# Layer 0 of a graph network: relations of three slots in four by matmul, a multiplied chunk last in each tile, and the tile's end ahead of the counts

## The chip, the cores and the metric

The kernel runs on one core of a Trainium2 chip. The metric is the device time of one launch in microseconds (us), as the median of several runs. Beside these runs there is one profiled execution, from which the trace and the profile page come. A measurement of the kernel before varies by about 0.3%.

## The reference, cut to what matters

Four graph layers follow one another on 3125 nodes of 128 features, with the same 100000 edges (src to dst), each layer added to its input and normalised. The change is in the first layer (L0), an attention over incoming edges whose logits and messages also depend on the type of the edge, one of 500 relations:

```python
z_bar = segment_sum(z[edge_type], dst) / max(deg, 1)
pre_edge = hP1[dst] + hP2[src] + zP3[edge_type]          # 128 wide
logit_edge = leaky(pre_edge) @ y_w                       # 8 heads
pre_self = hP1 + hP2 + z_bar @ P3;  logit_self = leaky(pre_self) @ y_w
alpha = softmax over self and incoming edges, per dst and head
t_edge = hWh[src] + zWz[edge_type];  t_self = hWh + z_bar @ Wz
out = leaky(segment_sum(alpha * t, dst) + residual_weight * h)   # h where deg == 0
```

Layer 1 is a mean over neighbours followed by two dense layers. Layers 2 and 3 are further attentions over the same edges.

## The kernel before, in words

**Tiles and slots.** Nodes are sorted by in-degree and cut into 25 tiles of 128 nodes, one node to a partition. Tile t has CAP[t] slots (57 in the first tile, 21 in the last, 821 in all); slot s of a tile holds the s-th incoming edge of each of its nodes. A chunk is W = 8 slots; the last chunk of a tile is shorter where CAP is not a multiple of 8.

**Gathers.** For each slot one indirect DMA on POOL (helper line L90) fetches 128 rows of `h_tab`, one per node: the row of the source node with its part of the pre-activation (128 columns), its message (128) and 8 logit columns, 264 f32 in all. They land in `hs`, a buffer of one chunk, of which there are eight. So a tile of four chunks has two generations of buffers.

**Two ways to the relation's part.** `gathered` (L820 to 835) fetches for each slot also 128 rows of `z_tab` by an indirect DMA into `zs` (328 columns, two buffers), adds `zs` to `hs` on DVE (L826), and sums the 64 raw relation columns by halving (L814, L817) into the tile's sum `za` (L828). `multiplied` (L837 to 875) fetches no relation rows. It loads the relation numbers of the chunk broadcast over the partitions (`rb`, 256 KB, a DMA on the SP queue, L843), compares them on DVE with the four blocks of relation ids (L852, `oh`, one-hot), multiplies the one-hots with the table of relations `zq` on PE (L854, `zps`), copies the product to `zT` on ACT (L856), and adds the relation's part by further matmuls: into `pre` (L858) and, by `t_ps` (L866), on DVE into `hs` (L867). The sum over the chunk's slots goes to `zbT` (L870 and the halving helper, L874). In both ways `pre` is completed by the node's own part (L799) and by transposes of the gathered rows (L833, L860), passed through a Relu on ACT (`low`, L806), and turned into logits by a small matmul for each slot (L808).

**Which chunks are multiplied.** `by_matmul(t)` takes about 45% of a tile's slots, in full chunks spread over the tile from slot 0 on; the tile's last chunk is a gathered one in most tiles. Over all tiles 47 chunks (376 slots) are multiplied and 445 slots have a `zs` gather.

**The end of a tile.** When all chunks have logits, `masked` adds the parts of the logits into `lgs` (L881, L882), `softmax` takes maximum, exponentials and sums (L680 to 692), `faded` (L697) rescales, and `spread` (L886 to 891) weighs each chunk's messages in its `hs` buffer, sums them by halving and adds them into `az`. Only then is an `hs` buffer free. After that come the node's own term, layer normalisation (L724 to 735) and the stores of `x1_tab` (POOL, L93) and `u_tab` (SP, L1008).

**The counts.** Between the chunks, a generator `counts` (L563 to 645) is advanced step by step. It builds, for layer 1, the matrix of edge counts of a tile: compares on DVE (L559 through the helper `one_hots`, L608), scalings on ACT (L612, L613), matmuls on PE (L616, L634), copies on ACT (L636) and a store on SP (L643). The main loop does not need its results.

**The order.** The Python loop issues the tiles one after another and, ahead of a tile's last chunk, the `prologue` of the next one (its `x` was fetched by `own` a tile earlier). A scheduler then lays out the instructions for each engine by priority, which follows the order of issue; each engine runs its own list in order. SP's list holds the loads of `rb`, of the tile's sums (L771) and the stores; POOL's list holds all gathers.

Of the kernel before, what the change touches and what calls it, by code (L numbers as in the profile page):

```python
# [18 lines left out]
P = 128  # L19
N = 3125  # L20
NT = 25
# [6 lines left out]
W = 8  # L28
# [5 lines left out]
H = 8  # L34
R = 64
HC = 2 * D + H
NK = (PADREL + 1) // P
# [3 lines left out]
CAP = [57, 42, 40, 39, 38, 37, 36, 35, 35, 34, 33, 33, 32, 31, 31, 30, 30, 29, 28, 28, 27, 26, 25, 24, 21]  # L41
assert len(CAP) == NT
OFF = [sum(CAP[:t]) for t in range(NT + 1)]
# [7 lines left out]
NB = [3] * 3 + [2] * (NT - 4) + [1]  # L51
CW = 512
NCW = -(-NP // CW)


def chunks(t):
    return [(s, min(W, CAP[t] - s)) for s in range(0, CAP[t], W)]
# [7 lines left out]
    return [(run[0][0], sum(run[-1]), run) for run in runs]  # L65


def by_matmul(t):

    full = CAP[t] // W  # L70
    n = (9 * CAP[t] + 10 * W) // (20 * W)
    return {i * full // n * W for i in range(n)}


@with_exitstack
def tile_gnn(ctx, tc, a, out):
# [409 lines left out]
    with tc.tile_pool(name="srcp", bufs=1) as sp, tc.tile_pool(name="srcq", bufs=2, space=PSUM) as ps:  # L486
# [28 lines left out]
        for o in range(0, NS, P):  # L515
            n = min(P, NS - o)
# [15 lines left out]
        blk0[nb] = late.tile([P, NT], F32, name=f"blk0_{nb}")  # L532
        G.iota(blk0[nb], pattern=[[nb * P, NT]], base=0, channel_multiplier=0, allow_small_or_imprecise_dtypes=True)
    SG = 8
    SE = max(NB) * CW // P
    each_j = slots.tile([P, NT, max(CAP)], BF16, name="each_j")
    V.tensor_copy(each_j, digits[:, :NT].unsqueeze(2).to_broadcast([P, NT, max(CAP)]))
    NAX = NT * max(NB)
# [16 lines left out]
    def one_hots(to, nums, n, up):  # L555

        for i, k, w in ((0, n // 2, 2), (n - n % 2, n % 2, 1)):
            if k:
                V.tensor_tensor(to[:, i // 2:i // 2 + k, :, :w], nums[:, i:i + k * w]  # L559
                                .rearrange("p (b w) -> p b w", w=w).unsqueeze(2).to_broadcast([P, k, P, w]),  # L560
                                up[:, :, :w].unsqueeze(1).to_broadcast([P, k, P, w]), op=OP.is_equal)

    def counts(t, cp, ps, up):  # L563
# [57 lines left out]
        cs = cp.tile([P, NP], BF16, name="c_sb")  # L621
        for c in range(NCW):
            w = min(CW, NP - c * CW)
            n2, e0 = nb * w // P, nb * CW // P * c
            yield
            ohs = cp.tile([P, SE // 2, P, 2], BF16, name="c_ohs", bufs=2)
            ohd = cp.tile([P, SE // 2, P, 2], BF16, name="c_ohd", bufs=2)
            for to, end in ((ohs, 0), (ohd, 1)):
                one_hots(to, ends[:, end, e0:e0 + n2], n2, up)
            cps = ps.tile([P, CW], F32, name="c_ps")  # L630
            for j in range(w // P):
                for i in range(nb):
                    b = nb * j + i
                    T.matmul(cps[:, j * P:(j + 1) * P], ohd[:, b // 2, :, b % 2], ohs[:, b // 2, :, b % 2],  # L634
                             start=(i == 0), stop=(i == nb - 1))
            A.activation(cs[:, c * CW:c * CW + w], cps[:, :w], AF.Copy)  # L636
        yield
        od_ps = ps.tile([P, NT], F32, name="c_od", tag="c_ps")
# [36 lines left out]
    def softmax(pool, lg, n, heads, m, l, ex=None):  # L675


        ex = lg if ex is None else ex
        mx = pool.tile([P, heads], F32, name="mx")
        V.tensor_reduce(mx, lg.rearrange("p s h -> p h s"), AX.X, OP.max)  # L680
        mn = pool.tile([P, heads], F32, name="mn")
        V.tensor_max(mn, m, mx)
        corr = pool.tile([P, heads], F32, name="corr")
        V.tensor_sub(corr, m, mn)
        A.activation(corr, corr, AF.Exp)
        V.tensor_copy(m, mn)
        V.tensor_sub(lg, lg, mn.unsqueeze(1).to_broadcast([P, n, heads]))
        A.activation(ex, lg, AF.Exp)
        sm = pool.tile([P, heads], F32, name="sm")
        V.tensor_reduce(sm, ex.rearrange("p s h -> p h s"), AX.X, OP.add)  # L690
        V.tensor_mul(l, l, corr)
        V.tensor_add(l, l, sm)
        return corr

    def faded(acc, corr, heads):
        acch = acc.rearrange("p (h d) -> p h d", h=heads)
        V.tensor_mul(acch, acch, corr.unsqueeze(2).to_broadcast([P, heads, D // heads]))  # L697
# [56 lines left out]
    with tc.tile_pool(name="l0", bufs=2) as wp, tc.tile_pool(name="l0s", bufs=1) as sp, \  # L754
# [82 lines left out]
        def multiplied(hq, o, n, zbT, first, lg_ps):  # L837

            hs = wp.tile([P, W, HC], F32, name="hs", bufs=8)
            for s in range(n):  # L840
                gather(hs[:, s, :], h_tab, srcx[:, o + s:o + s + 1])
            rb = wp.tile([P, W * P], F16, name="rb")
            nc.sync.dma_start(rb[:, :n * P], rel_tab[o:o + n].rearrange("(o s) p -> o (s p)", o=1)  # L843
                              .to_broadcast([P, n * P]))
            zT = wp.tile([P, W * P], F32, name="zT")
            for s0 in range(0, n, 4):
                k = min(4, n - s0)
                cols = slice(s0 * P, (s0 + k) * P)
                oh = wp.tile([P, NK, 4 * P], BF16, name="oh")[:, :, :k * P]
                zps = ps1.tile([P, 4 * P], F32, name="zps")[:, :k * P]  # L850
                for i in range(NK):
                    V.tensor_scalar(oh[:, i], rb[:, cols], relid[:, i:i + 1], None, op0=OP.is_equal)  # L852
                    for k2 in range(2):
                        T.matmul(zps, zq[:, i, 2 * R * k2:2 * R * (k2 + 1)], oh[:, i], start=(i + k2 == 0),  # L854
                                 stop=(i == NK - 1 and k2 == 1))
                A.activation(zT[:, cols], zps, AF.Copy)  # L856
                pre = argument(hq, k)
                T.matmul(pre[:, :k], zw[:, :D], zT[:, cols], start=False, stop=False)  # L858
                for s in range(k):
                    T.matmul(pre[:, s, :], hs[:, s0 + s, :D], ident, start=False, stop=(s == k - 1))  # L860
                logits(pre, k, lg_ps[:, s0:s0 + k])
            for s0 in range(0, n, 3):
                k = min(3, n - s0)
                t_ps = ps1.tile([P, 3, HC - D], F32, name="t_ps")
                for s in range(k):
                    T.matmul(t_ps[:, s, :], zT[:, (s0 + s) * P:(s0 + s + 1) * P], zw[:, D:], start=True, stop=True)  # L866
                V.tensor_add(hs[:, s0:s0 + k, D:], hs[:, s0:s0 + k, D:], t_ps[:, :k])  # L867
            assert n == W
            zh = wp.tile([P, W // 2, P], F32, name="zh")
            V.tensor_add(zh, zT.rearrange("z (s p) -> z s p", p=P)[:, :W // 2],  # L870
                         zT.rearrange("z (s p) -> z s p", p=P)[:, W // 2:])
            halved(zh, W // 2, zbT if first else None)
            if not first:
                V.tensor_add(zbT, zbT, zh[:, 0])  # L874
            return hs

        def masked(lg_ps, hss, n, mk):

            lg = wp.tile([P, max(CAP), H], F32, name="lgs")
# [37 lines left out]
        for t in range(NT):  # L917
# [5 lines left out]
            lg_ps = ps1.tile([P, max(CAP), H], F32, name="lg")  # L923
            zbT = wp.tile([P, P], F32, name="zbT")
            hss = []
            mults = by_matmul(t)
            for s0, w in chunks(t):
                o = OFF[t] + s0
                if s0 + w == n and t + 1 < NT:

                    ahead = x_next, prologue(t + 1, x_next)
                if s0 in mults:
                    hs = multiplied(hq, o, w, zbT, s0 == min(mults), lg_ps[:, s0:s0 + w])
                else:
                    hs = gathered(hq, lambda s: srcx[:, o + s:o + s + 1], rel[:, o:o + w], w, za, lg_ps[:, s0:s0 + w])
                hss.append((s0, w, hs))

                done += n_steps * w / NS
                while done > 0:
                    next(steps, None)  # L940
                    done -= 1
            lg = masked(lg_ps, hss, n, mask[:, OFF[t]:OFF[t + 1]])
            corr = softmax(wp, lg[:, :n], n, H, m[:, t, :], l[:, t, :])
            faded(ac, corr, H)
            for s0, w, hs in hss:
                spread(ac, hs, lg[:, s0:s0 + w], w)


            zaT_ps = ps1.tile([P, P], F32, name="tp", tag="misc")
# [420 lines left out]
```

## Time and profile before

| what | value |
|---|---|
| median of 3 runs | 4817.54 us (4814.24 to 4825.97) |
| the profiled execution, own time | 5636.56 us |
| its span | 5634.8 us, 37936 instructions |
| PE busy in the span | 2025.8 us (36%) |
| DVE busy | 2959.0 us (53%) |
| ACT busy | 927.9 us (16%) |
| POOL busy | 3069.7 us (54%) |
| gathers hs of layer 0 (L90) | 821, mean 1072 ns |
| gathers zs of layer 0 (L90) | 445, mean 1029 ns |
| data moved | 530.70 MB, 94 GB/s |

The profile page cuts the span in 40 slices of 141 us; each digit is an engine's busy share of a slice in tenths. The profile's views give, for a stretch of time, each engine's busy time, its instructions in order, or the waits: how long an engine stood idle ahead of an instruction, and which instruction released it. "issue" there means that nothing in the profile is seen to be waited for, and "remote" that the releasing event is not one that the profile can place.

### The profile page before, as it was taken

What the parts mean: (1) busy time and instruction counts of PE and PEld (TensorE: products, weight loads), DVE (VectorE), ACT (ScalarE), POOL (GpSimd) and SP (SyncE); (2) the same over time, 40 slices, a digit from 0 to 9 for tenths busy, and PEclk for the clock granted to TensorE, in tenths of its full rate; (3) what the DMA queues carried; (4) which work ended last, traced back from release to release, by engine and by line L of the source; (5) the groups of instructions that cost most, each with busy time, mean ns of one, the idle gap of its engine ahead of it and who ended that gap; (6) DMA issues with size and microseconds to landing.
All of it is one profiled execution on the core that took longest, in us unless ns stands there. A gap on an engine that the chain in (4) does not pass through costs nothing. (4 is left out here: it accounts for less than half of the span.)

```text
span 5634.8 us, 37936 instructions
## 1 busy us (share of the span) xinstructions
PE 2025.8 (36%) x10974; PEld 1311.2 (23%) x11061; DVE 2959.0 (53%) x6784; ACT 927.9 (16%) x2462; POOL 3069.7 (54%) x3137
## 2 busy tenths in 40 slices
PE   7164554556544555555564022222233100000000
PEld 5143433334333444334432010111111000000000
DVE  8354664555544655555432455555566354555555
ACT  1032222222222322222111011111111000000000
POOL 0545566454554445444503756666564476666665
PEclk9576766666676777776677555555555555555555
DMA  2423333332233333323343333333332233333322
GB/s 82 124 73 91 93 93 96 86 90 75 77 91 84 83 86 88 89 82 84 101 170 119 105 96 105 104 103 114 98 109 84 81 100 91 89 89 95 94 85 68
DMA packets 220244, 530.70 MB, mean 94 GB/s; under 512 B 65689, under 2 KB 112460, under 8 KB 215385
## 3 DMA queue, kind: packets, MB, share of 16 engines
q0 software_dynamic: 147968, 437.97, 27.6%
q1 hardware_dynamic: 72024, 89.90, 4.9%
q8 instruction: 94, 1.54, 0.1%
q14 instruction: 158, 1.29, 0.1%
HBM read 457.09 MB, written 70.63 MB: 94 GB/s over the span
## 5 line engine op out<-in xcount | busy, mean ns | idle before, releaser
L90 POOL DMA_INDIRECT hs<-h_tab,srcx x821 | 880.3, 1072 | 666.2 <-issue 534.7
L90 POOL DMA_INDIRECT kv<-kv_tab,pay_sb x821 | 783.6, 954 | 423.9 <-issue 241.1
L90 POOL DMA_INDIRECT kv<-ktv_tab,pay_sb x821 | 780.2, 950 | 336.0 <-issue 256.1
L90 POOL DMA_INDIRECT zs<-z_tab,rel x445 | 458.0, 1029 | 451.6 <-DVE az L828 141.6
L706 DVE TENSOR_REDUCE u<-msg 128x128 f32<-128x1024 f32 (+4 forms) x228 | 384.3, 1686 | 114.5 <-remote 61.6
L808 PE MATMUL lg<-yw,low 128*128 128x8 f32 x1642 | 243.5, 274 | 126.2 <-ACT low L806 72.2
L634 PE MATMUL c_ps<-c_ohs,c_ohd 128*128 128x128 bf16 x1300 | 139.5, 264 | 406.3 <-issue 193.9
L808 PEld LDWEIGHTS lg<-yw,low 128*128 128x128 f32 x1642 | 235.5, 218 | 173.0 <-ACT low L806 107.1
L1315 DVE TENSOR_TENSOR qk<-kv,qp 128x1024 f32<-128x1024 f32 (+4 forms) x114 | 126.5, 1110 | 279.4 <-DMA kv<-ktv_tab,pay_sb 257.4
L559 DVE TENSOR_TENSOR c_ohs<-c_ends,c_up 128x1024 bf16<-128x1024 bf16 (+4 forms) x178 | 113.2, 637 | 296.1 <-remote 251.0
L612 ACT ACTIVATE c_oha<-c_oha,srclo 128x50 bf16<-128x50 bf16 (+2 forms) x821 | 201.4, 327 | 355.6 <-DVE c_oha L608 270.1
L854 PE MATMUL zps<-oh,zq 128*128 128x512 bf16 x677 | 237.7, 466 | 49.4 <-DVE oh L852 21.4
L702 DVE TENSOR_TENSOR msg<-kv,ex 128x1024 f32<-128x1024 f32 (+4 forms) x228 | 249.3, 1105 | 0.0
L866 PE MATMUL t_ps<-zw,zT 128*128 128x136 f32 x752 | 153.3, 340 | 212.9 <-DVE hs L867 128.2
L1163 DVE TENSOR_TENSOR qk<-kv,qp 128x1024 f32<-128x1024 f32 (+4 forms) x114 | 126.1, 1107 | 183.2 <-DMA kv<-kv_tab,pay_sb 175.6
L634 PEld LDWEIGHTS <-c_ohd 128*128 128x128 bf16 x1300 | 114.0, 118 | 431.8 <-issue 333.0
L799 PE MATMUL pre<-identb,hq 128*128 128x512 bf16 (+3 forms) x645 | 203.3, 414 | 5.0 <-issue 4.1
L636 ACT ACTIVATE c_sb<-c_ps 128x512 bf16<-128x512 f32 (+1 forms) x175 | 96.3, 550 | 653.8 <-remote 441.9
L717 PE MATMUL tp<-ident,xk 128*128 128x128 f32 x100 | 43.6, 436 | 432.7 <-DVE xk L1231 131.2
L806 ACT ACTIVATE low<-pre 128x512 f32<-128x512 f32 (+1 forms) x215 | 123.1, 574 | 406.3 <-remote 140.3
L826 DVE TENSOR_TENSOR hs<-hs,zs 128x2112 f32<-128x2112 f32 (+7 forms) x67 | 132.6, 1979 | 102.9 <-issue 43.8
L866 PEld LDWEIGHTS t_ps<-zw,zT 128*128 128x128 f32 x752 | 130.1, 234 | 239.2 <-DVE hs L867 137.5
(398 smaller groups left out, 5183.8 us busy)
## 6 DMA issues: line engine op xcount, KB each, us to landing
c_tab<-c_sb SPq DMA_DIRECT2D x25, 768.0 KB
cs<-c_tab SPq DMA_DIRECT2D x6, 3200.0 KB
hs<-h_tab,srcx POOLq DMA_INDIRECT x821
kv<-kv_tab,pay_sb POOLq DMA_INDIRECT x821
kv<-ktv_tab,pay_sb POOLq DMA_INDIRECT x821
rb<-rel_tab SPq DMA_DIRECT2D x47, 256.0 KB
zs<-z_tab,rel POOLq DMA_INDIRECT x445
h_tab<-h SPq DMA_DIRECT2D x25, 132.0 KB
```

The source lines that it names most:

```text
L90: return G.indirect_dma_start(out=dst, out_offset=None, in_=table, in_offset=indirect(idx), **kw)
L612: A.activation(oha[:, s, 0, :], oha[:, s, 1, :], AF.Copy, scale=srclo[:, o:o + 1])
L634: T.matmul(cps[:, j * P:(j + 1) * P], ohd[:, b // 2, :, b % 2], ohs[:, b // 2, :, b % 2], start=(i == 0), stop=(i == nb - 1))
L702: V.tensor_tensor(msg[:, :n, :].rearrange("p s (h d) -> p s h d", h=heads), val.rearrange("p s (h d) -> p s h d", h=heads), ex.unsqueeze(3 ...
L706: V.tensor_reduce(u, msg[:, :n, :].rearrange("p s d -> p d s"), AX.X, OP.add)
L799: T.matmul(pre[:, :k], hq[:, i, :], identb.unsqueeze(1).to_broadcast([P, k, P]), start=(i == 0), stop=False)
L808: T.matmul(lg_ps[:, s, :], low[:, s, :], yw8, start=True, stop=True)
L826: V.tensor_add(hs[:, :n], hs[:, :n], zs[:, :n, :HC])
L854: T.matmul(zps, zq[:, i, 2 * R * k2:2 * R * (k2 + 1)], oh[:, i], start=(i + k2 == 0), stop=(i == NK - 1 and k2 == 1))
L866: T.matmul(t_ps[:, s, :], zT[:, (s0 + s) * P:(s0 + s + 1) * P], zw[:, D:], start=True, stop=True)
L1163: V.tensor_mul(qk[:, :n], kv[:, :n, :D], qp.unsqueeze(1).to_broadcast([P, n, D]))
L1315: V.tensor_mul(qk[:, :n], kv[:, :n, :D], qp.unsqueeze(1).to_broadcast([P, n, D]))
```

## The change

- `in_order(t)` takes the place of `by_matmul(t)`. It multiplies about three quarters of a tile's slots, n = (3 CAP + 16) // 32 chunks of the tile's first slots, and mixes the remaining chunks (the short one first) between them so that the last chunk of each tile is a multiplied one. A tile of 30 slots runs as: slots 24 to 29 gathered, then 0 to 7, 8 to 15 and 16 to 23 multiplied.
- In `multiplied` the one-hot compares of a chunk are four of 1024 columns, ahead of both halves, into six buffers, instead of eight of 512 columns, four in each half. The sum over the chunk's slots is one reduction instead of an addition and halvings.
- `softmax` is split into `weights` and a deferred `rest`; the exponentials of the logits come ahead of that of the correction.
- The end of a tile, from `masked` to `rest`, is issued with its priority raised by 600 places, ahead of what was issued before it, the counts among it.
- `counts` makes its one-hots in groups of eight blocks. This differs only where a tile has three blocks to a count tile (the first three tiles).

```diff
+AHEAD = 600
...
-def by_matmul(t):
-
-    full = CAP[t] // W
-    n = (9 * CAP[t] + 10 * W) // (20 * W)
-    return {i * full // n * W for i in range(n)}
+def in_order(t):
...
+    n = (3 * CAP[t] + 2 * W) // (4 * W)
+    mult = [(s, w, True) for s, w in chunks(t)[:n]]
+    rest = [(s, w, False) for s, w in chunks(t)[n:]][::-1]
+    k = len(mult) + len(rest)
+    return [(mult if (i + 1) * n // k > i * n // k else rest).pop(0) for i in range(k)]
...
+            for j0 in range(0, w // P, SG // nb):
+                tiles = range(j0, min(w // P, j0 + SG // nb))
+                e0, n2 = nb * (CW // P * c + j0), nb * len(tiles)
+                ohs = cp.tile([P, SG // 2, P, 2], BF16, name="c_ohs", bufs=2)
+                ohd = cp.tile([P, SG // 2, P, 2], BF16, name="c_ohd", bufs=2)
+                for to, end in ((ohs, 0), (ohd, 1)):
+                    one_hots(to, ends[:, end, e0:e0 + n2], n2, up)
...
-        A.activation(corr, corr, AF.Exp)
-        V.tensor_copy(m, mn)
         V.tensor_sub(lg, lg, mn.unsqueeze(1).to_broadcast([P, n, heads]))
         A.activation(ex, lg, AF.Exp)
-        sm = pool.tile([P, heads], F32, name="sm")
-        V.tensor_reduce(sm, ex.rearrange("p s h -> p h s"), AX.X, OP.add)
-        V.tensor_mul(l, l, corr)
-        V.tensor_add(l, l, sm)
-        return corr
+        A.activation(corr, corr, AF.Exp)
+
+        def rest():
+            V.tensor_copy(m, mn)
+            sm = pool.tile([P, heads], F32, name="sm")
+            V.tensor_reduce(sm, ex.rearrange("p s h -> p h s"), AX.X, OP.add)
+            V.tensor_mul(l, l, corr)
+            V.tensor_add(l, l, sm)
+
+        return corr, rest
...
+            ohs = []
+            for i in range(NK):
+                oh = wp.tile([P, W * P], BF16, name="oh", bufs=NK + 2)
+                V.tensor_scalar(oh[:, :n * P], rb[:, :n * P], relid[:, i:i + 1], None, op0=OP.is_equal)
+                ohs.append(oh)
...
-                oh = wp.tile([P, NK, 4 * P], BF16, name="oh")[:, :, :k * P]
...
-                    V.tensor_scalar(oh[:, i], rb[:, cols], relid[:, i:i + 1], None, op0=OP.is_equal)
...
-                        T.matmul(zps, zq[:, i, 2 * R * k2:2 * R * (k2 + 1)], oh[:, i], start=(i + k2 == 0),
+                        T.matmul(zps, zq[:, i, 2 * R * k2:2 * R * (k2 + 1)], ohs[i][:, cols], start=(i + k2 == 0),
...
-            zh = wp.tile([P, W // 2, P], F32, name="zh")
-            V.tensor_add(zh, zT.rearrange("z (s p) -> z s p", p=P)[:, :W // 2],
-                         zT.rearrange("z (s p) -> z s p", p=P)[:, W // 2:])
-            halved(zh, W // 2, zbT if first else None)
+            zh = zbT if first else wp.tile([P, P], F32, name="zh")
+            V.tensor_reduce(zh, zT.rearrange("z (s p) -> z p s", p=P), AX.X, OP.add)
             if not first:
-                V.tensor_add(zbT, zbT, zh[:, 0])
+                V.tensor_add(zbT, zbT, zh)
...
-            lg = masked(lg_ps, hss, n, mask[:, OFF[t]:OFF[t + 1]])
-            corr = softmax(wp, lg[:, :n], n, H, m[:, t, :], l[:, t, :])
-            faded(ac, corr, H)
-            for s0, w, hs in hss:
-                spread(ac, hs, lg[:, s0:s0 + w], w)
+
+            with tc.high_priority(offset=AHEAD):
+                lg = masked(lg_ps, hss, n, mask[:, OFF[t]:OFF[t + 1]])
+                corr, rest = weights(wp, lg[:, :n], n, H, m[:, t, :], l[:, t, :])
+                faded(ac, corr, H)
+                for s0, w, hs in hss:
+                    spread(ac, hs, lg[:, s0:s0 + w], w)
+                rest()
```

More of the change, by code (lines that the diff above doesn't have):

```diff
@@ L534, in tile_gnn @@
     SG = 8
-    SE = max(NB) * CW // P
     each_j = slots.tile([P, NT, max(CAP)], BF16, name="each_j")
@@ L623, in counts @@
             w = min(CW, NP - c * CW)
-            n2, e0 = nb * w // P, nb * CW // P * c
             yield
[L626 to L629, printed above, removed]
             cps = ps.tile([P, CW], F32, name="c_ps")
[L631 to L635, printed above, removed]
+            for j0 in range(0, w // P, SG // nb):
[5 more added lines that the diff above has]
+                    one_hots(to, ends[:, end, e0:e0 + n2], n2, up)
+                for j in tiles:
+                    for i in range(nb):
+                        b = nb * (j - j0) + i
+                        T.matmul(cps[:, j * P:(j + 1) * P], ohd[:, b // 2, :, b % 2], ohs[:, b // 2, :, b % 2],
+                                 start=(i == 0), stop=(i == nb - 1))
             A.activation(cs[:, c * CW:c * CW + w], cps[:, :w], AF.Copy)
@@ L675, in softmax, with weights @@
     def softmax(pool, lg, n, heads, m, l, ex=None):
+        corr, rest = weights(pool, lg, n, heads, m, l, ex)
+        rest()
+        return corr
+    def weights(pool, lg, n, heads, m, l, ex=None):
         ex = lg if ex is None else ex
@@ L925, in tile_gnn @@
             hss = []
-            mults = by_matmul(t)
-            for s0, w in chunks(t):
+            todo = in_order(t)
+            for i, (s0, w, mult) in enumerate(todo):
                 o = OFF[t] + s0
-                if s0 + w == n and t + 1 < NT:
+                if i + 1 == len(todo) and t + 1 < NT:
                     ahead = x_next, prologue(t + 1, x_next)
-                if s0 in mults:
-                    hs = multiplied(hq, o, w, zbT, s0 == min(mults), lg_ps[:, s0:s0 + w])
+                if mult:
+                    hs = multiplied(hq, o, w, zbT, s0 == 0, lg_ps[:, s0:s0 + w])
                 else:
@@ L941, in tile_gnn @@
                     done -= 1
-            lg = masked(lg_ps, hss, n, mask[:, OFF[t]:OFF[t + 1]])
-            corr = softmax(wp, lg[:, :n], n, H, m[:, t, :], l[:, t, :])
-            faded(ac, corr, H)
-            for s0, w, hs in hss:
-                spread(ac, hs, lg[:, s0:s0 + w], w)
+            with tc.high_priority(offset=AHEAD):
[4 more added lines that the diff above has]
+                    spread(ac, hs, lg[:, s0:s0 + w], w)
+                rest()
             zaT_ps = ps1.tile([P, P], F32, name="tp", tag="misc")
```

## Prediction

> **What bounds the kernel now.** I read the page's slices first, then windows, the POOL timeline and waits of the stage that the change touches.
>
> ```profile
> PE   7164554556544555555564022222233100000000
> DVE  8354664555544655555432455555566354555555
> POOL 0545566454554445444503756666564476666665
> ```
> A slice is 141 us. The first two are setup, slices 3 to 20 the main loop of layer 0 (about 249 to 2765 us, 2516 us, 25 tiles), then layer 1, then layers 2 and 3 from about 3010 us. The edit touches layer 0 alone. In its slices no engine passes six tenths.
>
> ```profile
> 300.00:2700.00 2400.00, 1307.33 (x8158) 938.61 (x8227) 1273.87 (x3398) 628.78 (x1703) 1268.92 (x1217) 0.69 0.32 87
> ```
> In this window the columns are busy time of PE, its weight load, DVE, ACT, POOL, then clock, DMA share and GB/s. PE, DVE and POOL are each at 53 or 54%; none is the bound by its busy time. So the timeline of POOL, one tile around 2086 us:
>
> ```profile
> 2085.59 0.95 POOL L90 DMA_INDIRECT hs<-h_tab,srcx  x1 [0.30 <-issue]
> 2086.54 0.22 POOL L776 MEMSET x<- 128x128 f32 x1
> 2087.03 1.01 POOL L90 DMA_INDIRECT x<-in_x,node_d  x1 [0.27 <-POOL x L776]
> 2095.66 1.03 POOL L93 DMA_INDIRECT x_tab<-x,node_d  x1 [7.61 <-DVE x L735]
> 2108.88 0.98 POOL L90 DMA_INDIRECT zs<-z_tab,rel  x1 [12.19 <-DVE az L828]
> ...
> 2126.64 0.95 POOL L90 DMA_INDIRECT zs<-z_tab,rel  x1 [0.30 <-issue]
> 2133.45 0.95 POOL L90 DMA_INDIRECT hs<-h_tab,srcx  x1 [5.87 <-issue]
> ```
> Start, duration, operation, and idle time before it. A gather is 0.95 us plus an issue gap of 0.30, so a pitch of 1.25 us. From the first hs gather of this burst (2047.88) to that of the next is 85.6 us. Of it some 31 hs gathers take 39, 14 zs gathers 18, the waits 7.61, 12.19 and 5.87 make 26. Other periods reach 98. POOL is thus occupied for about 60 us of a tile and stands behind buffers for the rest: zs has two buffers, released by the relation sums of an earlier chunk (L828), hs has eight, released by the weighted sums at a tile's end.
>
> ```profile
> ACT c_sb L636 <- remote: 425.2, 35, 27.5
> DVE c_ohs L559 <- remote: 248.8, 22, 35.5
> PE t_ps L866 <- DVE hs L867: 128.2, 22, 30.2
> POOL zs L90 <- DVE az L828: 121.8, 12, 19.1
> ```
> Waits in that window: total, times, longest. "Remote" here is PE's signal: the end of a group of L634 matmuls, recorded at 2148.55, is signalled at 2163.17. I can't say what holds it; all three compute engines are idle for some 700 us of the loop in such stretches, nearly all while POOL gathers. So compute and POOL hold each other up, and POOL is the more loaded chain.
>
> **What the Trainium skill says.** "Perfetto Trace Analysis", the section on a SWDGE DMA: a gather's recorded end is when its descriptors are written, not when its data lands. The trace agrees: hs rows of 264 columns and zs rows of 328 both have a median of 0.95 us. The price is for the instruction, whatever its bytes. "SBUF — State Buffer", Who interferes with whom: a two-port-mode DVE instruction and one with two SBUF inputs can block a gather. Half agrees: of 134 gathers over 1.1 us, 30 lie under L889 (50 us in all over 0.95 each) and 28 under L826 (39 us); 280 compares of L852 overlap gathers that stay at 0.95. "VectorE: DVE Perf Modes", side by side: a fixed part of about 150 cycles, then four 16-bit elements a cycle. The 512-column compare at 358 ns (L852) fits; by it the 1024-column one is an estimated 358 + 512/4/0.96 = 0.49 us.
>
> **The change part by part.**
>
> Relations. The chunk counts give 47 multiplied chunks before (3 in one tile, 2 in 20, 1 in four) and 77 after. So 240 zs gathers go (445 to 205) and 30 chunks change sides.
> - POOL: -240 x 1.25 = -301 us. At ten fewer per tile, the wait for zs buffers (121.8 us over 12) should mostly go too, since at most one or two gathered chunks are left to a tile.
> - PE: +30 x (16 zps + 4 pre<-zT,zw + 16 t_ps). By the rows' means (466, 785, 340 ns) that is 16 us a chunk, but these overlap; start-to-start they average 0.33, 0.66 and 0.20, so 11 us: +330 us over the loop. PE goes from 54 us a tile to 67 and becomes the most loaded compute engine.
> - DVE: a gathered chunk costs 3.5 (hs+zs 2.35, halvings 0.92, sum 0.22), of which 30 go: -105. A multiplied one was 6.1 (eight compares 2.86, hs+t_ps 1.58, sums 1.66) and becomes four compares 1.96, 1.58 and one reduction. The reduction of 1024 to 128 has no row in this stage; L706 has that shape with a median of 1.86 us, floor the 1.38 of the adds it replaces. I take 1.86 plus 0.28: 5.7. So 77 x 5.7 - 47 x 6.1 = +152, net +47, two a tile on an engine at 54%: hidden behind gathers, +47 if not.
> - ACT: +60 zT copies x 0.59 = +36, under its 26%.
> - SP: 30 more rb loads (256 KB). SP is a FIFO that waits 533.6 us at L843 for compares; behind it stand the loads of a tile's sums (L771), the stores of c_tab and of u_tab. A late sums load would hold the next tile's L828 and so its zs. DMA bytes fall: 240 x 168 KB less zs, 8 MB more rb, at a share of 0.32. Bounds: 0, as SP runs a tile ahead, to +3 us a tile.
>
> Compares first, six buffers of 1024 columns. DVE can run a chunk's four compares ahead of PE (cost above), PE no longer alternates with them. Bounds: -1 to +1 us a chunk; I take 0, as L854's wait on L852 is 21.4 us in all. The first zps now waits for a compare of 0.49 instead of 0.36.
>
> Order within a tile. The laid-out POOL order changes with it: before, zs of a tile follow its hs and x; after, a tile's few zs come ahead of its hs, while the last chunk, multiplied, needs no zs. The next tile's prologue goes ahead of that last chunk: its x load (memset, gather, 2.5 us on POOL), matmuls and hq are the same instructions, nothing added; its x must have come earlier by one chunk, and x is fetched a tile ahead, which hides it. If that cover goes, PE's FIFO waits up to 8 us with all of the chunk's matmuls behind it.
>
> Tile's end ahead of the counts. In the trace from the first lgs add to the first released hs buffer is about 22 us, with the count compares of L559 and L608 between. In the new DVE order these steps stand together with one or two count instructions in them: mask, maximum, differences, exp, one multiply of 1.22, halvings 0.68 + 0.42 + 0.28: about 8 us; the one exp table load a tile (L685, 1.28 us) stays. It moves no DMA; past it move the c_sb copies on ACT and the c_ps groups on PE, which only feed layer 1 and wait anyway. Gain 0 (buffers not on the path) to 14 us a tile; I take 2. The deferred m copy and l sum and the exp order are the same instructions, 0.
>
> Counts: three tiles get two 768-column compares where one of 1536 stood, in 6 full groups each: two more instructions a pair, 36 in all at about 0.15 us = +5 on DVE, taken as hidden (else +5).
>
> **Sum.** The profiled execution took 5636.56 us, its span 5634.8; the median of the runs is 4817.54, 819 us less. What that profile adds is not told by the page. Spread over its some 2,900 row gathers it is 0.28 us each, near the issue gap of 0.30, which would put the loop's 25 tiles at 86 us each outside a profile; if instead the late PE signals are the profile's, the loop is nearer 1,800 us, 72 a tile, with gathers at 1.25. Against the profiled time: -301 (POOL) - 50 (tile's end) + a third of PE's 330, exposed in stretches where POOL is not the later one, +110, -40 for zs waits = -280, so about 5355. Outside the profile at a pitch of 0.97 to 1.25: -233 to -301, and the same other terms, -215 to -280. I take **-247: 4570 us** (a saving of about 10 us a tile).
>
> **The rivals.**
> - *Both sides gain in full*: with short zs groups and early buffers POOL and compute overlap; the period falls from 86 to near the 67 of PE plus a few us, say 71: 15 x 25 = -375, 4440. For: the 26 us of waits in the shown period. Against: PE was stalled just as long.
> - *PE's queue takes most back*: as PE's 67 us with its waits for zT (0.59 us each) nears the period, the gain is 3 us a tile: 4740.
> - *PE becomes the bound, slower*: each chunk that turns from gathered to multiplied makes PE's FIFO go through zps, ACT's copy, pre, t_ps and DVE's add in turn, 16 us if nothing overlaps, against some 6 for a gathered one. If compute, not POOL, sets today's period, the 30 chunks cost 30 x 10 = +300, less what an earlier tile's end gives (0 to 250): I take +100, 4920. It decides from the point where PE's in-order time per tile passes today's period of 72 to 86 us; 67 plus stalls of 5 to 20 is near it. For: t_ps waits 128.2 us on DVE. Against: compute sits idle while POOL gathers.
> - *It does not do what it says*: POOL spends freed time waiting for hs buffers, because the tile's end comes no earlier: within 14 us, 4810.
>
> **Numbers.** About 0.3% (14 us) is what a measurement of this kernel can tell from no change. Main case 0.48, full gain 0.20, most given back 0.13, no effect 0.05, slower 0.14. That is faster 0.81, same 0.05, slower 0.14. The range leaves out half of the slower case and the best part of the full gain: 4370 to 4850.
>
> **What would show it.** zs x205, rb x77, POOL busy down by about 230 (240 x 0.95); hs bursts every 70 to 80 us of profile; "zs <- az L828" under 30 us; oh as 128x1024 near 0.49 us; the reduction near 1.86; PE busy in the loop up by about 330 and its clock above 0.69. Wrong would be: hs waits that grow by what zs gave up, PE or weight-load waits on zT or oh in the hundreds of us, or SP's L771 behind L843 holding zs. Layers 2 and 3 should not move.

## The result, and the profile after

The changed kernel takes 4855.48 us (4854.79 to 4857.68, 4 runs) where the kernel before takes 4818.69: a ratio of 1.0076, 95% interval 1.0058 to 1.0093. It is slower by 37 us where the prediction had 247 us less.

On some chips of this study the kernel before takes about 4818 us, on others about 5600 to 5650, in every run, and its first trace was from one of the latter; each kernel is therefore compared with the kernel before on its own chip only. The trace of the changed kernel is from the first kind: its profiled execution took 4857.68 us, as long as the other runs.

The slices of the page, now of 121 us each:

```profile
PE   7365678777767776677660222233333000000000
DVE  8555669675677666685324656566674465555556
POOL 0447547676574545364017777777772777777776
```
PE and DVE stand a tenth or two higher than before in slices 3 to 19, POOL about where it was. In the window of 300 to 2200 us (busy time of PE, its weight load, DVE, ACT, POOL, then clock, DMA share, GB/s):

```profile
300.00:2200.00 1900.00, 1345.91 (x8873) 961.80 (x8990) 1315.57 (x3245) 636.25 (x1700) 1114.44 (x982) 0.80 0.34 93
```
PE is at 71%, DVE at 69%, POOL at 59%. Still no engine is full. The last `lgs` mask of the loop is at 2315 us. From the first hs gather at 205 us to 2317 us, just behind that mask, the loop takes 2112 us, 84.5 a tile. Everything behind it takes 2539 us; by the same rest the kernel before, on this kind of chip, ends its loop near an estimated 4816 - 2539 = 2277 us, 83 a tile.

The timeline of POOL at the seam of two tiles (rows left out at the dots):

```profile
1489.09 5.03 POOL L94 DMA_INDIRECT hs<-h_tab,srcx  x1 [13.06 <-issue]
...
1531.93 0.95 POOL L94 DMA_INDIRECT hs<-h_tab,srcx  x1 [0.30 <-issue]
1532.88 0.22 POOL L790 MEMSET x<- 128x128 f32 x1
1533.37 1.02 POOL L94 DMA_INDIRECT x<-in_x,node_d  x1 [0.27 <-POOL x L790]
1534.70 1.03 POOL L97 DMA_INDIRECT x_tab<-x,node_d  x1 [0.30 <-issue]
1536.03 0.97 POOL L94 DMA_INDIRECT zs<-z_tab,rel  x1 [0.30 <-issue]
...
1542.32 0.94 POOL L94 DMA_INDIRECT zs<-z_tab,rel  x1 [0.30 <-issue]
1576.69 5.03 POOL L94 DMA_INDIRECT hs<-h_tab,srcx  x1 [33.43 <-PE pre L877]
```
There are six zs gathers instead of 14, no wait ahead of them, and then 33.43 us in which POOL stands before the next hs burst. At this seam the waits of 7.61, 12.19 and 5.87 us of the trace before (of the other kind of chip) have become one that is longer than their sum. The pitch of a gather is still 1.25 us. Over the whole loop POOL stands 477 us ahead of hs gathers, the gap of 0.30 us that every gather has taken off.

What the longer wait depends on is seen on DVE. Its timeline, same seam:

```profile
1479.41 0.42 DVE L897 TENSOR_TENSOR lgs<-lgs,mask 128x256 f32<-128x256 f32 x1
...
1509.89 2.08 DVE L840 TENSOR_TENSOR hs<-hs,zs 128x1848 f32<-128x1848 f32 x1
...
1545.84 0.36 DVE L828 TENSOR_TENSOR zs<-zs 128x192 f32<-128x192 f32 x1 [25.68 <-DMA zs<-z_tab,rel]
1546.11 0.57 DVE L884 TENSOR_TENSOR hs<-hs,t_ps 128x408 f32<-128x408 f32 x1
...
1566.18 0.41 DVE L897 TENSOR_TENSOR lgs<-lgs,mask 128x248 f32<-128x248 f32 x1
```
L897 is the mask with which a tile's end begins. A slot has 8 columns there, so the two masks are those of a tile of 32 slots and of one of 31: tiles 12 and 13, counted from 0. L840 is the hs+zs add of a gathered chunk, here of 7 slots; it is tile 14's. L828 is here the first sum of raw relation columns, of a chunk of six slots; counted through the list it is that of tile 16, whose hs rows are gathered only from 1662 us on. Both stand ahead of tile 13's mask in DVE's list, and DVE runs its list in order. The sum waits 25.68 us for zs gathers that POOL issues behind the whole hs burst of tile 14. PE and ACT run dry meanwhile: nothing is busy on them from 1524 to 1544 us.

Waits of DVE for gathers in the loop (total us, times, longest):

```profile
DVE zs L828 <- DMA zs<-z_tab,rel: 156.6, 10, 25.7
DVE hs L840 <- DMA hs<-h_tab,srcx: 129.8, 12, 31.9
DVE hs L840 <- DMA zs<-z_tab,rel: 92.0, 5, 23.6
DVE zs L831 <- DMA zs<-z_tab,rel: 31.6, 2, 18.4
```
In all 410 us. The waits close a ring: the end of tile 12 (mask at 1479.41) frees hs buffers; the hs burst of tile 14 runs from 1489.09, with x and zs gathers behind it to 1543.3; DVE's early sum follows at 1545.84, then the rest of tile 13 to its mask at 1566.18, and from there the next burst at 1576.69. From mask to mask that is 10 + 54 + 3 + 20 = 87 us, the period.

The same can be counted in DVE's list, which is laid out with the program and is the same on every chip. In the kernel before, the first gathered add of a tile stands behind the mask of the tile ahead of it in 19 of 24 cases, and 8 to 30 rows ahead of it in five. In the changed kernel it stands ahead in 23 of 24, by 10 to 115 rows; the early sum shown above stands 42 rows ahead of the mask.

### The profile page after: what moved, and what is told of

Read it like the earlier page. It is cut to its first block, busy times and chain, and to the rows that moved or that the text cites. A ratio compares the mean times of both kernels' runs of the same rounds, so it can differ in the third digit from the quotient of the medians.

```text
span 4855.9 us, 39698 instructions
## 1 busy us (share of the span) xinstructions
PE 2085.6 (43%) x12000; PEld 1357.0 (28%) x12141; DVE 2996.6 (62%) x6658; ACT 954.2 (20%) x2522; POOL 2914.1 (60%) x2897
## 5 line engine op out<-in xcount | busy, mean ns | idle before, releaser
L883 PE MATMUL t_ps<-zw,zT 128*128 128x136 f32 x1232 | 236.1, 324 | 268.8 <-DVE hs L884 266.9
L871 PE MATMUL zps<-oh,zq 128*128 128x512 bf16 x1103 | 333.9, 416 | 34.3 <-DVE oh L862 24.3
L94 POOL DMA_INDIRECT zs<-z_tab,rel x205 | 234.0, 1142 | 103.2 <-issue 57.3
L883 PEld LDWEIGHTS t_ps<-zw,zT 128*128 128x128 f32 x1232 | 201.3, 220 | 306.4 <-DVE hs L884 286.7
L840 DVE TENSOR_TENSOR hs<-hs,zs 128x2112 f32<-128x2112 f32 (+7 forms) x37 | 62.1, 1678 | 264.4 <-DMA hs<-h_tab,srcx 145.8
L877 PEld LDWEIGHTS pre<-ident,hs 128*128 128x128 f32 x1232 | 174.5, 207 | 85.0 <-issue 56.4
L875 PE MATMUL pre<-zT,zw 128*128 128x512 f32 x308 | 184.0, 682 | 33.0 <-ACT zT L873 32.4
L877 PE MATMUL pre<-ident,hs 128*128 128x128 f32 x1232 | 184.3, 293 | 24.3 <-DMA hs<-h_tab,srcx 24.3
L820 ACT ACTIVATE low<-pre 128x512 f32<-128x512 f32 (+2 forms) x215 | 122.8, 573 | 330.8 <-PE pre L877 205.0
L1251 PE MATMUL p_ps<-wqkv,xkT 128*128 128x384 f32 x200 | 158.5, 895 | 45.9 <-ACT xkT L733 45.9
```

The source lines that it names most:

```text
L94: return G.indirect_dma_start(out=dst, out_offset=None, in_=table, in_offset=indirect(idx), **kw)
L871: T.matmul(zps, zq[:, i, 2 * R * k2:2 * R * (k2 + 1)], ohs[i][:, cols], start=(i + k2 == 0), stop=(i == NK - 1 and k2 == 1))
L1251: T.matmul(p_ps, xkT, wqkv[:, k, :], start=(k == 0), stop=(k == NTY - 1))
```

## The experiments

Three theories were held in turn. A: DVE's list waits for zs gathers behind an hs burst. B: the in-order work of PE and DVE sets the period, as in the prediction's rival. C: the ring above, through the early add and the early sums together. Four kernels ran on a chip where the kernel before takes 4818; these decide most.

**The 240 gathers put back.** Each turned chunk of the changed kernel issues its zs gathers all the same, into two buffers of one row that nothing reads:

```diff
                 gather(hs[:, s, :], h_tab, srcx[:, o + s:o + s + 1])
+                if extra:
+                    zx = wp.tile([P, HC + R], F32, name="zx", bufs=2)
+                    gather(zx, z_tab, rel[:, o + s:o + s + 1])
```


> The changed kernel, with the 240 zs gathers that it saves issued all the same, into two one-row buffers that nothing reads. If gathers on POOL set the period, as the prediction had it: 240 x 1.25 = 300 us above the changed kernel, or at least 150. Theory B (PE's and DVE's in-order work sets it, POOL waits): within 60 us of the changed kernel.

Measured: 5067.49 us, ratio to before 1.0523 (1.0505 to 1.0540), 212 us above the changed kernel. But the scheduler did not leave these gathers in their chunks. Since nothing reads them, all 240 came early, the last at 1176 us:

```profile
L94 POOL DMA_INDIRECT zx<-z_tab,rel x240: 940/946/16980, 193.5 to 1176.4; - x120
```
Tile 7's mask comes at 1268 us instead of 1050; from there to the last mask both kernels take the same time (1264 and 1265 us). So POOL's time is on the path in the first eight tiles, and nothing is said of the others. Nor is 212 us the price of 240 gathers, as they wait 85 us for each other's two buffers.

**The 240 gathers taken away alone.**

```diff
-                gather(zs[:, s, :], z_tab, rl[:, s:s + 1])
...
+                if not none:
+                    gather(zs[:, s, :], z_tab, rl[:, s:s + 1])
+            if none:
+                V.tensor_add(hs[:, :n], hs[:, :n], nosum[:, :1].unsqueeze(2).to_broadcast([P, n, HC]))
+            else:
+                V.tensor_add(hs[:, :n], hs[:, :n], zs[:, :n, :HC])
...
```


> The kernel before, with the zs gathers of the 30 chunks left out and nothing in their place (240 gathers fewer): these chunks add zeros to hs, and leave out their relation sums (30 x 1.1 us of DVE). Their relation part is left out of the result. If POOL sets the period: 200 to 300 us below before. Theory B: 0 to 80 us below before.

Measured: 4411.85 us, ratio 0.9159 (0.9144 to 0.9175), -406 us: more than 240 x 1.25 = 300. Waits for zs buffers probably go with them, and DVE's list is laid out anew; how much is due to each is not shown. (The edit also takes 33 us off DVE.) DVE's waits for gathers in its loop:

```profile
DVE hs L828 <- DMA hs<-h_tab,srcx: 49.9, 7, 12.8
DVE hs L830 <- DMA hs<-h_tab,srcx: 38.9, 5, 15.9
DVE hs L830 <- DMA zs<-z_tab,rel: 16.6, 1, 16.6
```
L828 is in this kernel the add of zeros, L830 the hs+zs add. 105 us, against 410 in the changed kernel. POOL stands 101 us ahead of hs gathers in this loop, against 477. So the gain that the prediction counted on can be had, and between this kernel and the changed one 444 us are lost. Both have the same 205 zs gathers; but here the gathered chunk is the last of most tiles, and its add stands 45 to 133 rows behind the mask of the tile ahead. In tiles 13 to 19 the changed kernel takes 579 us and this one 412. DVE is busy there for 371 and 349 us, PE for 394 and 339; POOL's waits for hs buffers are 208 and 37. So in these tiles the loss of 167 us is about what POOL waits longer.

**The counts left out, of both kernels.** Zeros are stored to the counts' table ahead of the loop instead, so layer 1 of these two kernels gets no sums.

```diff
-        steps = all_counts()
+        steps = iter(())
...
                 while done > 0:
-                    next(steps, None)
                     done -= 1
```


> The changed kernel with the counts left out: zeros are stored to c_tab ahead of the loop, so layer 1 gets no sums. Takes about 14 us a tile off PE, 15 off DVE and 14 off ACT, nothing off POOL. Theory B: 250 to 450 us below the changed kernel. If POOL or the hs buffers set the period: under 120 us below it.

Measured: 4854.91 us. That is the changed kernel's time to the microsecond, although a third of DVE's work in the window below and half of ACT's is gone. Window of 600 to 2000 us, of the changed kernel and then of this one:

```profile
600.00:2000.00 1400.00, 1009.08 (x6628) 721.43 (x6717) 980.76 (x2423) 480.13 (x1294) 819.96 (x720) 0.81 0.34 92
```
```profile
600.00:2000.00 1400.00, 893.32 (x4735) 616.54 (x4806) 655.32 (x1689) 238.65 (x485) 789.61 (x721) 0.80 0.30 82
```
DVE falls from 70 to 47%, ACT from 34 to 17%, PE from 72 to 64%, and the loop as a whole doesn't shorten, so in-order compute alone doesn't set the pace. But the equal times are luck. Tile 12's mask comes 67 us later than in the changed kernel, and from there to the last mask this kernel takes 63 us less. Why its first tiles are slower is open; DVE's list is another one there. What its later tiles gain can be read term by term. The seam shown above, in this kernel (rows of DVE and of POOL):

```profile
1546.19 0.42 DVE L897 TENSOR_TENSOR lgs<-lgs,mask 128x256 f32<-128x256 f32 x1
1556.31 5.04 POOL L94 DMA_INDIRECT hs<-h_tab,srcx  x1 [24.43 <-issue]
1609.51 0.97 POOL L94 DMA_INDIRECT zs<-z_tab,rel  x1 [0.30 <-issue]
1613.08 0.62 DVE L828 TENSOR_TENSOR zs<-zs 128x192 f32<-128x192 f32 x2 [30.39 <-DMA zs<-z_tab,rel]
1625.07 0.41 DVE L897 TENSOR_TENSOR lgs<-lgs,mask 128x248 f32<-128x248 f32 x1
```
Means of tiles 13 to 19, in us:

| | mask to hs burst | hs burst to end of zs | to DVE's sum | sum to next mask | period |
|---|---|---|---|---|---|
| changed kernel | 9.5 | 50.0 | 2.3 | 20.9 | 82.8 |
| without counts | 8.9 | 49.7 | 2.3 | 12.2 | 73.1 |

The compute behind DVE's sum falls by 8.7 us and the period by 9.7; POOL's stretch stays. So in these seven tiles the terms follow one another as theory C has it: POOL's burst and DVE's rest take turns. DVE's own waits for gathers grow meanwhile, in the loop:

```profile
DVE hs L840 <- DMA hs<-h_tab,srcx: 391.0, 29, 32.5
DVE zs L828 <- DMA zs<-z_tab,rel: 346.2, 26, 30.4
DVE hs L840 <- DMA zs<-z_tab,rel: 58.1, 2, 31.2
DVE zs L831 <- DMA zs<-z_tab,rel: 27.7, 2, 25.2
```
823 us, twice those of the changed kernel, at the same instructions: what becomes faster outside the ring only waits longer at the gathers.

> The kernel before with the counts left out in the same way (layer 1 gets no sums). Theory B: compute sets the period there too, 250 to 400 us below before until POOL's 60 us a tile stop it. If POOL sets the period in the kernel before: under 120 us below it. In both theories it should fall by less than the changed kernel does, since POOL has 10 us more a tile.

Measured: 4767.95 us, ratio 0.9899 (0.9883 to 0.9916), -50 us, with DVE's L826 waiting 550.8 us for zs in 600 to 2000 us.

```profile
600.00:2000.00 1400.00, 774.86 (x4267) 548.89 (x4325) 633.70 (x1939) 228.83 (x475) 1058.67 (x952) 0.76 0.39 105
```
POOL is busy for 1059 us of this window, and its 933 gathers and scatters have a gap of 0.30 us each, an estimated 280 us more: 96% of the window, against 74% in the changed kernel. So with the counts gone POOL's serial gathers hold this kernel, as the prediction read it. DVE's list changed here too: the first gathered add of a tile stands 1 to 8 rows ahead of the mask in 16 of 24 cases, where the kernel before has five. So the 50 us are not what the counts cost by themselves.

The other kernels ran on chips where the kernel before takes about 5630.

**The kernel before once more, for its trace.**

> The kernel before once more, for its trace: the first profiled execution of it was 819 us longer than the runs, that of the changed kernel was not. Both theories: 4818 us within 14. If the late PE signals of the first trace belonged to the profile, a profiled execution as long as the runs has none of them, a gather pitch still of 1.25 us, and the loop of layer 0 near 83 us a tile.

Measured: 5638.02 us where the kernel before takes 5634.31, ratio 1.0005; its profiled execution took no longer than the other runs. So nothing of the 819 us belonged to the profile, and the expected 4818 us missed. On these chips PE's signals do come late. In this kernel's loop 158 of them come more than 3 us after the last recorded end of a matmul, and over a hundred in each of the 14 other traces of such chips; in the five traces of the first kind none does. That the late signals are the whole of the difference is not shown.

**The changed kernel there.**

> The changed kernel once more, beside the kernel before on the same chip. The last four kernels ran where the kernel before takes 5634 us and PE's signals come late, as in its first trace; the result was measured where it takes 4818. Theory A and B alike: 1.008 of before where before takes 4818. Where it takes 5634, PE's late signals add to every wait for PE; with one more of them for each of the 30 added chunks it would be 1.01 to 1.03, without that 0.99 as the two variants of it that ran there.

Measured: 5599.78 us, ratio 0.9909 (0.9879 to 0.9940): on such a chip the change gains 0.9%. While POOL gathers (gathers less than 0.5 us apart taken as one stretch), PE is busy 42% of the time there, and 80% of the time otherwise; in the other trace 65 and 87%. Gathers and compute go together less well on these chips, which may be why fewer gathers help there. DVE's waits for gathers are only 93 us: it waits for PE's late signals first.

**Its parts.** The tile's end raised in the kernel before; not raised in the changed kernel; the relations alone:

```diff
-            with tc.high_priority(offset=AHEAD):
+            if True:
```


> The kernel before with the tile's end alone (masked, softmax, faded, spread, unsplit) at 600 places higher priority. Theory A: hs buffers come free about 10 us earlier in each tile, and hs bursts set zs and so compute: 100 to 250 us less than before, 4570 to 4720. Theory B: compute sets the period, within 20 us of 4818.

> The changed kernel without the raised priority of the tile's end; all else as changed. Theory A: each hs burst starts some 10 us later, and the zs behind it too: 100 to 250 us more than 4855. Theory B: within 30 us of 4855.

> The changed kernel without the raised priority of the tile's end. Theory C: the tile's end is a part of the ring, so it grows by some 10 us a tile: 100 to 250 us above 4855. If the raised priority is what pulls the next tile's zs sums and adds ahead of this tile's chunks in DVE's list, it falls instead: 50 to 200 us below.

> The kernel before with in_order alone: 77 multiplied chunks, 205 zs gathers, the last chunk multiplied; eight compares of 512 columns, tile's end and counts as before. By the prediction's sum, 240 gathers less at 1.25 us against PE's added work: 150 to 250 us below before. Theory A: the gain is lost to zs waits, within 60 us of the changed kernel and within 1% of before. Theory B: the 30 chunks add more than the gathers give, 0 to 100 us above before.

> The kernel before with in_order alone. Theory C: its gathered chunk comes first in each tile too, so the ring is there, with an unraised tile's end: 4850 to 5000. By the prediction's sum: 4570 to 4670.

Measured: the raised end alone 1.0197 (1.0165 to 1.0229), slower; the changed kernel without it 0.9898 and 0.9883, no different from the changed kernel with it; the relations alone 0.9925 and 0.9930. So on these chips the relations make some three quarters of the gain of 0.9%, though the intervals overlap. Theory A's range for the relations alone was met (within 1% of before and 60 us of the changed kernel); the other ranges, set for the other kind of chip, were not. Why a raised end costs 2% in the kernel before was not followed up. The lists of these kernels say one thing for both kinds of chip: with the relations' new order alone, and without the raised end, the first gathered add stands ahead of the mask in 23 of 24 cases. So the relations' edit puts it there, not the raised end.

**Every chunk multiplied.**

> The changed kernel with every chunk of every tile multiplied, short ones too: no zs gather is left, 110 multiplied chunks. Theory A: no zs wait on DVE is left; PE adds about 33 x 8 us and the waits of some 280 us go: -50 to +50 us against the changed kernel. Theory B: PE and DVE do another 33 chunks in the period that they set: 150 to 330 us above the changed kernel.

Measured: 5679.07 us, 1.0054 (1.0036 to 1.0071), 79 us above the changed kernel beside it. 33 chunks more cost 2.4 us each net of their gathers: between the two expectations.

**The ring cut.** First the relation sums behind their add, by a factor 1 that depends on it; then with the gathered chunk second in the tile as well; last, add and sums behind the end of the tile before (the lines shown are the last one's):

```diff
+                one = wp.tile([P, 1], F32, name="one")
+                V.tensor_scalar(one, after[:, 0, 0:1], 0.0, 1.0, op0=OP.mult, op1=OP.add)
+                V.scalar_tensor_tensor(hs[:, :n], hs[:, :n], one, zs[:, :n, :HC], op0=OP.mult, op1=OP.add)
...
```


> The changed kernel, with the sums of the raw relation columns of a gathered chunk made to depend on that chunk's hs+zs add, so that they can't stand 250 rows ahead of it in DVE's list. Theory A (DVE's FIFO waits for zs gathers that stand on POOL behind a whole burst of hs gathers, 280 us in all, and this took the gain): 190 to 280 us less than the changed kernel, 4580 to 4665. Theory B (the in-order work of PE and DVE, 60 us each of 84 a tile, sets the period; the waits would only move): within 40 us of 4855.

> The changed kernel with the relation sums behind the hs+zs add, beside the changed kernel itself. Theory A (DVE's list waits for zs gathers behind an hs burst): 190 to 280 us below the changed kernel. Theory B (PE's and DVE's in-order work sets the period): within 40 us of it.

> The changed kernel with the relation sums behind their hs+zs add, now hoped for where the kernel before takes 4818 us. Theory C (a ring sets the changed kernel's period: tile's end, hs burst of 33 us, the zs gathers behind it on POOL, DVE's early relation sums that wait for them ahead of the other tile's work, tile's end): 100 to 300 us below the changed kernel's 4855. If the ring closes by the early hs+zs add (L840) as well, less than 100.

> The changed kernel with the relation sums behind their add and the gathered chunk second in the tile instead of first, so that no gathered chunk of the next tile stands among this tile's last chunks on DVE. Theory C: the ring is opened, 250 to 400 us below the changed kernel, 4450 to 4600, near the 4412 of the kernel before with 240 gathers fewer. If in-order compute is the pace after all: within 60 us of 4855.

> The changed kernel, with a gathered chunk's hs+zs add and relation sums made to depend on the end of the tile before (a factor 1 made from its weights). In DVE's list that add then stands some 40 rows behind the last tile's mask instead of 56 ahead of it; POOL, PE and ACT have the same work. Theory C (ring: tile's end, hs burst, this add and the zs sums, the other tile's end): 250 to 400 us below the changed kernel where that takes 4855, so 4450 to 4600. If in-order compute is the pace: within 60 us. Where PE's signals come late (before at 5634), these would hide part: 50 to 300 us below 5600.

> The changed kernel with the gathered chunk's add and relation sums behind the end of the tile before, once more. Where the kernel before takes 4818 us, theory C (the ring through the early add and sums) has it 250 to 400 us below the changed kernel, 4450 to 4600; in-order compute as the pace has it within 60 us of 4855. Where the kernel before takes about 5620, 1.03 of it as in its first run, which says nothing on the ring.

Measured: the sums behind the add 0.9910, 0.9879 and 0.9892 (5583.90 us beside the changed kernel's 5599.78); gathered chunk second 0.9915; both behind the tile's end 1.0295 and 1.0249, slower. All of these ran on chips with late signals, where DVE waits only 93 us for gathers in the changed kernel, so they neither support nor refute theory C for the measured result; theory A's gain of 190 us is not there on such chips. In the first two kernels the add itself still stands ahead of the mask in most tiles (23 and 22 of 24), so neither cuts the whole ring. The last does move the add to some 40 rows behind the mask, and is worse here: POOL then waits 719 us for hs buffers in a window of 2000 us (446 in the changed kernel on such a chip, the gap of 0.30 us taken off in both), perhaps because compute that could run beside the burst comes later.

## Why the prediction was wrong, point by point

- **What bounds the kernel before** was right, as far as the runs tell: POOL's serial gathers. Taking 240 of them away gives -406 us, and without the counts POOL is occupied for 96% of the window and the time falls by 50 us only. A trace of the kernel before itself on a chip of the first kind is missing.
- **The gathers' term**, -301 us with -40 for zs waits, was too small by 65 as a term by itself (-406, of which up to 33 may be DVE's).
- **Instruction prices** held: 1024-column compares 494 ns (0.49 estimated with the Trainium skill's "VectorE: DVE Perf Modes", side by side), the reduction 1.91 us (1.86), zps 416 ns, first hs gather 9.7 us after the mask (8). The tile's end does stand together. What held of the page is the slope: its fixed part would give an estimated 0.29 us for 512 columns, where the rows have 0.36.
- **The step that failed is "Order within a tile".** It looked at POOL's list, and costed the move of the gathered chunk to the front of the tile, and of the prologue, at nothing. It did not count DVE's list. With the gathered chunk last in the tile, as in the kernel with 240 gathers fewer, its add stands behind the end of the tile ahead. With it first, the scheduler puts the add, and the sums of a tile later still, in front of the mask that frees the hs buffers. There they wait for zs gathers that POOL issues behind an hs burst: 410 us in the loop. Behind the waiting instruction stand the hs+t_ps adds of the tile in work, and for those wait PE's t_ps (228.5 us in the window), ACT, and in the end POOL, with 477 us ahead of its hs gathers against 101 in the kernel with 240 gathers fewer. The added wait was put at zero.
- **A third of PE's 330 us exposed** was the wrong kind of cost. PE's union rose, but PE waits; with the counts left out it is busy 116 us less in the window of 600 to 2000 us, and the total stays.
- **The rival "It does not do what it says"**, at 0.05, had the place right: POOL spends the freed time waiting for hs buffers. So did the stated sign of being wrong, hs waits that grow. Its reason, that the tile's end comes no earlier, was not the one: the tile's end itself took 9.7 us, near the 8 counted on, but the mask came late.
- **The slower rival** had the sign at 0.14, but as PE's queue with 16 us a chunk. In tiles 13 to 19 of the kernel without counts the period falls by what DVE's list loses behind its sum, which speaks against PE's queue there. The mechanism that acted was a wait on an engine that none of the rivals named.
- **The base** was shaky: the 819 us between profile and median were spread over gathers, at a pitch of 0.97 outside the profile. The pitch is 1.25 in runs of 4855 us too; the trace came from another kind of chip than the times. Nor did all of the 819 us lie in layer 0: behind its last mask, at 2828 us and not at 2765 where its gathers end, that trace has 2807 us, against 2539 here. The loop's 83 us a tile came out near the 86 assumed by chance.
- **The reading of lengthened gathers** was loose: of the compares of L852 in that loop 264 lie over a gather, and 167 of them over none longer than 1.0 us. What the trace shows more plainly stands in the last section.

What is shown: the gathers' gain can be had (-406); the relations' edit puts adds and sums of later tiles ahead of the mask, where with the gathered chunk last they stand behind it; DVE waits 410 us for gathers at these instructions; and in tiles 13 to 19 POOL's burst and DVE's rest take turns, term by term, in two kernels. These tiles account for 167 of the 444 us. What is argued: that the same waits account for the rest. DVE's waits in the whole loop exceed those of the kernel with fewer gathers by 410 - 105 = 305 us, POOL's for hs buffers by 376; the added chunks' own work may be a part. The kernels that take the sums, or sums and add, out of the ring ran on chips of the second kind alone. So whether such a version beats both on the first kind stays open.

## What to carry to other kernels

When work is moved within a tile, a scheduler can move its consumers forward in an in-order list: after such a change, look for instructions of a later tile that stand ahead of the one that frees the buffers, and ask what their data wait for. A cost per instruction says nothing about that; the place in the list does. The same holds for an experiment: look in its trace where the added or removed work really stood, and compare stretch by stretch, as two equal totals can hide a loss and a gain. And before a trace is used to predict a time, compare its own length with the runs: 17% apart meant another state of the machine here, not a scale factor.

## What the runs showed of the hardware

- On some chips PE's completion signals came late, up to tens of us (one t_ps of the changed kernel with a recorded end at 1439.46 us was signalled at 1463.02); 79 to 84% of the late time lay in POOL's gather stretches, which took 58 to 68% of the loop. The kernel before took about 5600 to 5650 instead of 4818 us there, and the change had the opposite sign (0.9909 against 1.0076).
- Gathers that follow one another without a wait have a pitch of 1.25 us on both kinds, 0.95 of it the instruction. Those that no DVE instruction overlapped took at most 1.04 us (628 in the loop of the kernel before, 356 in that of the changed one). Those that overlapped the hs+zs add, which has two inputs in SBUF, had a median of 1.77 us (51 gathers); those that overlapped one-hot compares alone, 0.95 us (25 gathers).
- A reduction of 1024 f32 columns to 128 on DVE with a stride of 128 took 1.91 us, more than the three adds of 1.38 in all that it replaced.
